# A four-layer graph network: seven groups of four dense and three listed node tiles in place of eight of four and two

## The chip, the core and the metric

The kernel runs on one core of a Trainium2 chip. The engines that matter are PE (TensorE, the matmuls; its weight loads are shown as PEld), DVE (VectorE), ACT (ScalarE), POOL (GpSimd, which here issues every gather and scatter) and SP (SyncE, which issues the plain loads and stores). The metric is the device time of one launch in microseconds (us), the median over several runs.

## The reference

A graph of 6,250 nodes with 128 features and 100,000 edges, sorted by destination, passes through four message-passing layers, each with a residual and a layer norm. The change touches the first and the third.

```python
# first layer
msg = x[src]
summed = jax.ops.segment_sum(msg, dst, num_segments=n)
mean = summed / jnp.maximum(cnt, 1.0)[:, None]
out = mean @ W_l + b_l + x @ W_r
...
# third layer: five steps of a gated unit, state h of 256 features
def step(h, Wl):
    m = h @ Wl
    agg = jax.ops.segment_sum(m[src], dst, num_segments=n)
    gi = agg @ w_ih.T + b_ih
    gh = h @ w_hh.T + b_hh
    ...
    r = jax.nn.sigmoid(ir + hr)
    z = jax.nn.sigmoid(iz + hz)
    ng = jnp.tanh(in_ + r * hn)
    h_new = (1.0 - z) * ng + z * h
    return (h_new, None)
h, _ = jax.lax.scan(step, h, W)
```

The sum over edges, `segment_sum(m[src], dst)`, is the costly part: six times in all, once for `x` and five times for the growing state.

## The kernel before

The 6,250 nodes are padded to 49 tiles of 128. A sum over edges is made for each tile of destination nodes in one of two ways.

- **Dense.** Four tiles (512 destination nodes) are one group. Its adjacency, 49 source tiles by 512 columns, is counted once in the first layer (`subtile`, line 872: one-hot matmuls in strips of U = 12 destination nodes, copied by ACT into `stage`) and kept in DRAM as bf16 (`adj_d`). A sum is then 49 matmuls of 512 columns for each part of the source table. In the first layer there are three bf16 parts (`dense0`, line 899, matmul at L904). In the third layer the table is held as two fp32r halves, for one block of 128 features in the first of the five steps and two in the others (`dense2`, line 1355, matmul at L1366): 98 matmuls in that first step and 196 in the others. The adjacency comes back from DRAM two source tiles at a time (`ab_load`) and ACT casts it to fp32r (`ab_cast`, L1337).
- **Listed.** One tile's edges lie in a list of SLOTS = 18 slots of 128 edges. For each slot POOL gathers the 128 source rows from DRAM (`gather`, L751), DVE makes a one-hot of the destinations (L1388), and one matmul adds them (`sparse0`, L935; `sparse2`, L1398). The gathers run AHEAD = 6 slots in advance in the third layer, into seven buffers. A gathered row is 2 KB there (1 KB in the first of the five steps), and 768 bytes in the first layer.

`steps` lists the chunks in node order: four dense tiles, two listed tiles, eight times, and tile 48 alone as a listed one. So 32 tiles are dense in eight groups and 17 are listed, in nine chunks.

The third layer (lines 1297 to 1597) is called the gated stage below, and its five steps are its layers 0 to 4. After the sum of a chunk come its gates (`gates`, fp32 matmuls at L1450, 48 per chunk in layers 1 to 4 and half of that in layer 0, as wide as the chunk), then the chunk's new state is turned back to rows (`rows`) and stored into the next layer's table `tab`. A gather of the next layer waits for all of that table. The weights that mix W and w_ih, `wf`, are loaded per layer (`wf_load`) into one of two buffers. The source table `hs` is reloaded in seven pieces as the last dense group of a layer finishes with each (`hs_load`).

The order of work is written by hand. Each action gets a time, `play` sorts the actions by it, and the instructions go onto every engine's queue in that order. One unit of that time is one dense group, called a round here: T = 8 rounds per layer. In the gated stage, within a layer:

- dense group d runs from d to d + 1, its gates from d + 1.005 to d + 1.305, its rows from d + 1.36;
- the listed slots start at S0 = 0.6 (0 in layer 0) and run at 36 slots per SR = 0.9 rounds (0.93 in layer 0); a listed chunk's gates come 0.05 to 0.17 after its last slot;
- the records of the fourth graph layer are scattered to DRAM by POOL as filler (`scatter`, L1535, 782 in all): from layer 1 on behind four of every seven slots, and BETWEEN = 30 behind the last slots of each layer but the last, each of these after a small memset;
- `wf` of the next layer is loaded at 6.5, the last piece of `hs` at 8.5, and the gathers of the next layer start at 8 + 0.55.

The first layer is pipelined in the same way: while group d's adjacency is counted, group d - 1 is summed by `dense0`, the listed slots run beside both, and `post` makes the layer's output rows for each chunk.

Of the kernel before, what the change touches and what calls it, by code (L numbers as in the profile page):

```python
# [15 lines left out]
P = 128  # L16
# [643 lines left out]
def even(ctx: ExitStack, tc: tile.TileContext, a, out, rec_d, start_d, list_d, rc):  # L660
# [32 lines left out]
    steps = [r for t in range(0, NT - 1, 6) for r in (range(t, t + 4), range(t + 4, t + 6))] + [range(NT - 1, NT)]  # L693
    dense, sparse = steps[0:16:2], steps[1::2] + steps[16:]
# [81 lines left out]
    with tc.tile_pool(name="f0", bufs=1) as l0, \  # L776
# [34 lines left out]
        for i, ts in enumerate(sparse):  # L811
# [3 lines left out]
            for j in range(len(ts)):  # L815
                for to, k in ((src_l, 0), (dst_l, 1)):
                    nc.sync.dma_start(to[:, 2 * i + j, :], list_d[k, bass.ds(at[j], SLOTS * P)]
                                      .rearrange("(p s) -> p s", p=P))
        first_l = l0.tile([P, len(listed)], F32, name="first_l")
        nc.gpsimd.iota(first_l[:, :16], pattern=[[6 * P, 8], [P, 2]], base=4 * P, channel_multiplier=0,  # L820
                       allow_small_or_imprecise_dtypes=True)
        nc.gpsimd.memset(first_l[:, 16:], float((NT - 1) * P))
# [11 lines left out]
        each = -(-DW // U)  # L834
        blocks = [(d, ts[0] * P // U + u, min(SU, each - u)) for d, ts in enumerate(dense) for u in range(0, each, SU)]
# [36 lines left out]
        def subtile(d, b, u, after):  # L872
# [6 lines left out]
            w = min(U, DW - c)  # L879
            p = ps(f"adj_p{b}_{u}", "adj", 2, 1024)  # L880
            for j, ohk in enumerate(hot.pop((b, u))):
                for q in range(2):
                    nc.tensor.matmul(p[:, q * 512:q * 512 + KH * U], ohss[b][:, 2 * u + j, :],  # L883
                                     ohk[:, q * KH * U:(q + 1) * KH * U], start=(j == 0), stop=(j == 1))
            nc.scalar.copy(stages[d][:, :, c:c + w].rearrange("p (q b) d -> p q b d", q=2),  # L885
                           p.rearrange("p (q n) -> p q n", q=2)[:, :, :KH * U]
                           .rearrange("p q (b d) -> p q b d", d=U)[:, :, :, :w])
# [53 lines left out]
        def turned0(t):  # L941
            ts = steps[chunk_of[t]]
            if t == ts[0]:
                aggT[ts] = l0.tile([P, 2 * P], F32, tag="aT0s", bufs=2, name=f"aT0s_{t}")
# [5 lines left out]
        def post(ts, at, by):  # L950
# [8 lines left out]
            def load():  # L959
                h["xr"] = xr = l0.tile([P, 4, D], F32, tag="xr", bufs=3, name=f"xr{r0}")  # L960
                if ts[-1] == NT - 1:
                    nc.vector.memset(xr[:, m - 1, :], 0.0)
                    nc.sync.dma_start(xr[:last, m - 1, :], a["x"][(NT - 1) * P:N, :])
                else:
# [68 lines left out]
        with tc.manual_schedule(engines=FOUR):  # L1033
# [13 lines left out]
            for d in range(len(dense)):  # L1047
# [14 lines left out]
                events += post(dense[d], d + 2.02, d + 2.95 if d < 7 else d + 2.5)  # L1062
            for k in range(len(hots)):
                t = 0.3 + 8.2 * (k + 0.5) / len(hots)
                events.append((t, lambda k=k: sparse0(k)))
                i, j = hots[k]
                if j == SLOTS - 1:
                    events.append((t + 0.05, lambda i=i: turned0(listed[i])))
                    ts = steps[chunk_of[listed[i]]]
                    if listed[i] == ts[-1]:  # L1070
                        events += post(ts, t + 0.08, t + 1.0 if i < 13 else t + 0.6)

            for c in range(NC3):
                w0, w1 = (c * K3 + KFULL, (c + 1) * K3) if c < NC3 - 1 else (c * K3, W3)
                events.append((0.5 + c * 0.5, lambda w0=w0, w1=w1: nc.sync.dma_start(
# [223 lines left out]
    with tc.tile_pool(name="f2", bufs=1) as l2, \  # L1299
# [14 lines left out]
        BETWEEN = 30  # L1314
# [6 lines left out]
        def ab_load(layer, d, g):  # L1321
            if g >= NG2:
                layer, d, g = (layer, d + 1, g - NG2) if d < 7 else (layer + 1, 0, g - NG2)
# [6 lines left out]
        def ab_cast(layer, d, g):  # L1330
            if g >= NG2:
                layer, d, g = (layer, d + 1, g - NG2) if d < 7 else (layer + 1, 0, g - NG2)
# [18 lines left out]
        def wf_load(layer):  # L1351
            wfs[layer] = wf = l2.tile([P, 2, 6 * D], F32, tag="wf", bufs=2, name=f"f_wf{layer}")
# [878 lines left out]
```

## Time and profile before

| | us |
|---|---|
| median of the runs | 7822.81 (7804.96 to 7860.64, 3 runs) |
| the profiled execution, its own time | 6785.85 |
| its span, first to last instruction | 6784.0 |
| mean granted TensorE clock in it | 0.925 |

The profiled execution stands 13% below the median of the runs; nothing in the span accounts for that. The stages lie in the span as follows:

| stage | from | to | granted clock |
|---|---|---|---|
| preparation | 0 | 150 | 1.00 |
| first graph layer | 150 | 895 | 0.93 to 0.99 |
| second graph layer | 895 | 1990 | 0.69 |
| gated stage (third graph layer) | 1990 | 5540 | 0.97 |
| its output layers, fourth graph layer | 5540 | 6784 | 0.97 |

In the gated stage, POOL starts the first and the last gather of each layer at these times:

| layer | first gather | last gather | between them | to the next layer's first |
|---|---|---|---|---|
| 0 | 1961.3 | 2418.3 | 457 | 65 |
| 1 | 2482.8 | 3208.4 | 726 | 56 |
| 2 | 3264.5 | 3980.8 | 716 | 57 |
| 3 | 4037.5 | 4764.9 | 727 | 57 |
| 4 | 4821.8 | 5516.4 | 695 | |

To read the groups of the profile: a line is the engine's line of code, operation, output and inputs by name, number of instructions, then their busy time, the mean of one in ns, and the idle time of the engine just before them with what ended it. [...] the time of one there is longer than the distance from one to the next.

### The profile page before, as it was taken

The numbers are of one execution on the slowest core, as the hardware profiler recorded it, in microseconds if no ns is written. First come the engines' busy times: TensorE is split into PE (matmuls) and PEld (weight loads), VectorE is DVE, ScalarE is ACT, GpSimd is POOL, SyncE is SP. The second block draws the span as 40 slices with busy tenths as digits, with TensorE's granted clock in tenths as the row PEclk, the third lists the DMA queues.
The fourth block names the chain that finished last, engine by engine and source line by source line (L and its number), as shares of the span: only waits on it lengthen the run. The fifth ranks groups of instructions, "written<-read, shape, count | busy, mean of one in ns | idle before, by whom it ended". The sixth has DMA issues, their size and how long they took to land.

```text
span 6784.0 us, 83554 instructions
## 1 busy us (share of the span) xinstructions
PE 5785.0 (85%) x25602; PEld 4010.0 (59%) x25758; DVE 2946.3 (43%) x8835; ACT 2406.6 (35%) x3623; POOL 4264.2 (63%) x4426
## 2 busy tenths in 40 slices
PE   0699977788859989999999989999899987888888
PEld 0355546555546657666676667666676665665665
DVE  7666634466624422222222222222222235677766
ACT  0344411111116543333333333333333323444444
POOL 3555447777756656656666666666666622777776
PEclk9999976777759999999999999999999998999999
DMA  5688744444458888778777787778777743444443
GB/s 172 162 235 244 252 139 143 140 133 137 125 170 267 264 294 258 247 226 290 255 254 232 246 294 255 242 228 298 229 239 220 230 153 101 105 108 107 110 107 82
DMA packets 804250, 1355.75 MB, mean 200 GB/s; under 512 B 165854, under 2 KB 429139, under 8 KB 802771
## 3 DMA queue, kind: packets, MB, share of 16 engines
q1 hardware_dynamic: 555219, 698.41, 32.4%
q0 software_dynamic: 207472, 568.37, 28.0%
q10 hardware_dynamic: 41104, 83.51, 3.2%
q8 instruction: 211, 3.46, 0.2%
q14 instruction: 244, 2.00, 0.1%
HBM read 1046.51 MB, written 303.32 MB: 199 GB/s over the span
## 4 chain that ended last, share of the span: by engine, by line
PE 39%; DMA 13%; POOL 4%; DVE 4%; issue 3%; ACT 1%; SPq 0%; DVEq 0%; ACTq 0%; POOLq 0%
PE ag_p L1366 16%; DMA m<-tab,src_l 5%; PE r L1450 5%; DMA f_m<-by_dst,f_ix 5%; PE z L1450 5%; PE sp_p L1398 4%; PE h L1450 2%; POOL f_m L751 2%; PE i L1450 2%; POOL rec_d L1535 1%; DVE f_m L1734 1%; PE f_y_p L1623 1%; DMA ab<-adj_d 1%; DMA rec_d<-f_rec,row 1%; PE s_p L1822 1%
## 5 line engine op out<-in xcount | busy, mean ns | idle before, releaser
L1366 PE MATMUL ag_p<-af,hs 128*128 128x512 f32 x7056 | 2105.0, 422 | 82.5 <-DMA ab<-adj_d 35.6
L751 POOL DMA_INDIRECT m<-tab,src_l x1530 | 1479.5, 967 | 1061.9 <-PE ag_p L1366 483.9
L1366 PEld LDWEIGHTS ag_p<-af,hs 128*128 128x128 f32 x7056 | 1329.3, 194 | 493.4 <-issue 136.3
L1337 ACT CAST af<-ab 128x1024 fp32r<-128x1024 bf16 (+1 forms) x1000 | 1023.2, 1028 | 990.5 <-PE ag_p L1366 636.9
L751 POOL DMA_INDIRECT f_m<-by_dst,f_ix x819 | 795.4, 971 | 304.1 <-issue 225.5
L751 POOL DMA_INDIRECT fm<-f_hw,turned_hw x782 | 781.6, 1000 | 247.0 <-issue 97.5
L1535 POOL DMA_INDIRECT rec_d<-f_rec,row x782 | 778.3, 995 | 236.9 <-issue 206.2
L1398 PE MATMUL sp_p<-m,s 128*128 128x512 f32 (+1 forms) x1530 | 685.0, 448 | 168.1 <-DMA m<-tab,src_l 162.7
L1388 DVE TENSOR_SCALAR s<-iota_h,loc_l 128x128 fp32r<-128x128 f16 x1530 | 420.7, 302 | 778.2 <-PE sp_p L1398 774.9
L1287 PE MATMUL sum<-fs,fm 128*128 128x128 f32 (+13 forms) x1924 | 453.4, 373 | 205.2 <-DMA fm<-f_hw,turned_hw 138.7
L751 POOL DMA_INDIRECT m<-x_in,src_l x306 | 356.5, 1165 | 339.8 <-PE sp_p L935 153.7
L1287 PEld LDWEIGHTS sum<-fs,fm 128*128 128x128 f32 x1924 | 368.3, 266 | 322.4 <-DVE fs L1278 133.1
L1398 PEld LDWEIGHTS sp_p<-m,s 128*128 128x128 f32 x1530 | 296.0, 193 | 345.0 <-issue 197.4
L883 PE MATMUL adj_p<-ohk,ohs 128*128 128x300 bf16 x1376 | 240.3, 298 | 121.8 <-DMA recs<-rec_d 83.8
L1464 DVE SCALAR_TENSOR_TENSOR r<-h,fc_b_hh,r 128x256 f32<-128x256 f32 (+2 forms) x170 | 101.7, 600 | 518.8 <-PE h L1450 466.2
L904 PE MATMUL ag_p<-stage,xs 128*128 128x512 bf16 x1116 | 312.0, 388 | 16.3 <-DMA xs<-x_in 8.9
L1781 ACT ACTIVATE f_hs<-dT,fc_eb 128x512 f32<-128x512 f32 (+1 forms) x208 | 148.8, 715 | 498.9 <-DVE dT L1779 498.9
L885 ACT CAST stage<-adj_p 128x600 bf16<-128x600 f32 (+1 forms) x344 | 224.8, 655 | 267.2 <-PE adj_p L883 263.3
L1472 ACT ACTIVATE z<-z,f_brz 128x256 f32<-128x256 f32 (+2 forms) x170 | 96.7, 569 | 597.9 <-PE z L1450 535.5
L1257 ACT COPY f_rec<-ap_p 128x512 f32<-128x512 f32 x196 | 105.2, 589 | 555.6 <-issue 336.6
L1481 DVE TENSOR_TENSOR r<-hold,ng 128x256 f32<-128x256 f32 (+2 forms) x153 | 84.4, 552 | 461.9 <-ACT ng L1474 460.1
L1278 DVE TENSOR_SCALAR fs<-f_iota_n,loc,turned_wgt 128x128 f32<-128x128 f32 x782 | 243.8, 355 | 94.7 <-PE sum L1287 93.9
(368 smaller groups left out, 8966.5 us busy)
## 6 DMA issues: line engine op xcount, KB each, us to landing
ab<-adj_d SPq DMA_DIRECT2D x960, 256.0 KB
f_rec<-edge_d SPq DMA_DIRECT2D x391, 130.0 KB
rg<-rec_d SPq DMA_DIRECT2D x195, 260.0 KB
edge_d<-f_rec SPq DMA_DIRECT2D x97, 520.0 KB
adj_d<-stage SPq DMA_DIRECT2D x8, 6272.0 KB
tab<-r ACTq DMA_DIRECT2D x196, 256.0 KB
hs<-tab SPq DMA_DIRECT2D x28, 1792.0 KB
xs<-x_in SPq DMA_DIRECT2D x56, 672.0 KB
```

The source lines that it names most:

```text
L751: nc.gpsimd.indirect_dma_start(out=dst, out_offset=None, in_=table, in_offset=bass.IndirectOffsetOnAxis(ap=idx, axis=0))
L883: nc.tensor.matmul(p[:, q * 512:q * 512 + KH * U], ohss[b][:, 2 * u + j, :], ohk[:, q * KH * U:(q + 1) * KH * U], start=(j == 0), stop=(j ...
L885: nc.scalar.copy(stages[d][:, :, c:c + w].rearrange("p (q b) d -> p q b d", q=2), p.rearrange("p (q n) -> p q n", q=2)[:, :, :KH * U] .rea ...
L904: nc.tensor.matmul(sums["d", d], parts[d, g][:, s % XG, q, :], stages[d][:, s, :], start=(s == 0 and q == 0), stop=(s == NT - 1 and q == 2))
L1278: nc.vector.tensor_scalar(s, iota_n, loc[:, k:k + 1], wgt[:, k:k + 1], op0=ALU.is_equal, op1=ALU.mult)
L1287: nc.tensor.matmul(sums[c][:, x0 - c0:x1 - c0], msg, s[:, x0 - w0:x1 - w0], start=False, stop=(k == last_k[c]))
L1337: nc.scalar.copy(af[:, :m, :], abs_.pop((layer, d, g))[:, :m, :])
L1366: nc.tensor.matmul(sums[layer, d, k], hs[:, s, q, k, :], afs[layer, d, g][:, s % SG, :], start=(s == 0 and q == 0), stop=(s == NT - 1 and ...
L1388: nc.vector.tensor_scalar(s, iota_h, loc_l[:, i, j:j + 1], None, op0=ALU.is_equal)
L1398: nc.tensor.matmul(p[:, :2 * w], hot.pop((layer, k)), msgs.pop((layer, k))[:, :2 * w], start=(j == 0), stop=(j == SLOTS - 1))
L1450: nc.tensor.matmul(p[:, :n], w[:, k, ms], src, start=(start and i == 0), stop=(stop and i == len(ks) - 1))
L1535: st = nc.gpsimd.indirect_dma_start(out=rec3_d, out_offset=bass.IndirectOffsetOnAxis(ap=row3[:, c:c + 1], axis=0), in_=recs[c // CB][:, c ...
```

## The change

The groups become seven, of four dense and three listed tiles each. 7 times 7 is 49, so no tile is left over: 28 tiles are dense in seven groups, 21 are listed in seven chunks. The schedule's constants follow: T is 7 rounds, 54 slots per 0.948 rounds (1.0 in layer 0), a scatter behind every second slot, 24 scatters between layers. A group now starts at a node that is no multiple of 12, so the strips of `subtile` are cut at both ends of the group; seven groups have 303 strips, eight had 344. The tiles of the listed chunks grow from two to three node tiles. `wf` has one buffer in place of two and is loaded at 7.6, which is 0.6 rounds into the next layer, behind the last gates of the layer before. `first_l`, `tiles_i` and the loading of the last rows of `x` are rewritten for the new groups.

```diff
-    steps = [r for t in range(0, NT - 1, 6) for r in (range(t, t + 4), range(t + 4, t + 6))] + [range(NT - 1, NT)]
-    dense, sparse = steps[0:16:2], steps[1::2] + steps[16:]
+    steps = [r for t in range(0, NT, 7) for r in (range(t, t + 4), range(t + 4, t + 7))]
+    dense, sparse = steps[0::2], steps[1::2]
...
-        each = -(-DW // U)
-        blocks = [(d, ts[0] * P // U + u, min(SU, each - u)) for d, ts in enumerate(dense) for u in range(0, each, SU)]
+        blocks = []
+        for d, ts in enumerate(dense):
+            b0, b1 = ts[0] * P // U, -(-(ts[0] * P + DW) // U)
+            blocks += [(d, b, min(SU, b1 - b)) for b in range(b0, b1, SU)]
...
-            w = min(U, DW - c)
+            c0, c1 = max(c, 0), min(c + U, DW)
...
             for k in range(len(hots)):
-                t = 0.3 + 8.2 * (k + 0.5) / len(hots)
+                t = 0.3 + 7.2 * (k + 0.5) / len(hots)
...
-                events.append((0.5 + c * 0.5, lambda w0=w0, w1=w1: nc.sync.dma_start(
+                events.append((0.5 + c * 0.4, lambda w0=w0, w1=w1: nc.sync.dma_start(
...
-        BETWEEN = 30
+        BETWEEN = 24
...
-            wfs[layer] = wf = l2.tile([P, 2, 6 * D], F32, tag="wf", bufs=2, name=f"f_wf{layer}")
+            wfs[layer] = wf = l2.tile([P, 2, 6 * D], F32, tag="wf", name=f"f_wf{layer}")
...
-        S0, SR = 0.6, 0.9
+        S0, SR = 0.6, 0.948
...
-            T = 8
+            T = 7
...
-                    add(o + 8.5, lambda layer=layer: hs_load(layer + 1, 6))
-                    add(o + 6.5, lambda layer=layer: wf_load(layer + 1))
+                    add(o + 7.5, lambda layer=layer: hs_load(layer + 1, 6))
+                    add(o + 7.6, lambda layer=layer: wf_load(layer + 1))
                 s0 = S0 if layer else 0.0
-                per = SR if layer else 0.93
+                per = SR if layer else 1.0
...
-                    t = o + s0 + per * (k + 0.5) / 36
+                    t = o + s0 + per * (k + 0.5) / 54
...
-                    if layer and k % 7 in (0, 2, 4, 6) and k + AHEAD < len(hots) and scattered < NK:
+                    if layer and k % 2 == 0 and k + AHEAD < len(hots) and scattered < NK:
...
-                        add(o + s0 + per * 8.32 + 0.4 * k / BETWEEN, lambda c=scattered: scatter(c, True))
+                        add(o + s0 + per * 6.83 + 0.4 * k / BETWEEN, lambda c=scattered: scatter(c, True))
```

## The prediction

> **What bounds the kernel now.** I read the page's engine shares and stage windows first, since the change touches two stages, then the groups, then the timeline of POOL and PE.
>
> ```profile
> PE 5785.0 (85%) x25602; PEld 4010.0 (59%) x25758; DVE 2946.3 (43%) x8835; ACT 2406.6 (35%) x3623; POOL 4264.2 (63%) x4426
> ...
> L751 POOL DMA_INDIRECT m<-tab,src_l x1530 | 1479.5, 967 | 1061.9 <-PE ag_p L1366 483.9
> L1535 POOL DMA_INDIRECT rec_d<-f_rec,row x782 | 778.3, 995 | 236.9 <-issue 206.2
> ```
>
> By busy time PE looks like the bound and POOL looks free. The idle column corrects that: the 782 scatters have 236.9 us of idle before them, 0.30 us each, and nothing ended it ("issue"). The timeline shows that this gap is part of the price:
>
> ```profile
> 2151.66 0.95 POOL L751 DMA_INDIRECT m<-tab,src_l  x1 [0.30 <-PE r L1450]
> 2152.92 0.95 POOL L751 DMA_INDIRECT m<-tab,src_l  x1 [0.30 <-issue]
> 2154.17 0.94 POOL L751 DMA_INDIRECT m<-tab,src_l  x1 [0.30 <-issue]
> ...
> 2648.13 0.97 POOL L751 DMA_INDIRECT m<-tab,src_l  x1 [0.30 <-PE ag_p L1366]
> 2649.41 0.99 POOL L1535 DMA_INDIRECT rec_d<-f_rec,row  x1 [0.30 <-issue]
> 2650.70 0.97 POOL L751 DMA_INDIRECT m<-tab,src_l  x1 [0.30 <-DMA m<-tab,src_l]
> ```
>
> Starts are never closer than 1.25 us (gathers alone) or 1.28 (gathers with scatters). Now the rounds, as windows:
>
> ```profile
> core 0: us, PE busy (x) PEld busy (x) DVE busy (x) ACT busy (x) POOL busy (x), PEclk, DMA share, GB/s
> 418.50:501.00 82.50, 75.93 (x413) 43.26 (x420) 57.33 (x176) 39.65 (x69) 43.90 (x38) 1.00 0.83 244
> 2151.00:2202.00 51.00, 46.50 (x199) 32.45 (x198) 23.59 (x70) 33.55 (x46) 36.09 (x39) 1.00 0.84 271
> 2514.00:2605.00 91.00, 88.80 (x353) 64.05 (x352) 26.48 (x73) 34.95 (x46) 62.96 (x65) 1.00 0.78 254
> 2985.00:3089.00 104.00, 96.61 (x380) 68.74 (x380) 27.63 (x76) 36.27 (x50) 64.81 (x66) 1.00 0.73 232
> ```
>
> First graph layer (row 1): 38 x 1.25 = 48 of 82.5 us on POOL; PE leads. Gated layer 0 (row 2): 39 x 1.25 = 49 of 51; POOL is the bound. Layer 1 (row 3): 65 x 1.28 = 83 of 91 on POOL, PE 89 of 91; both nearly full. Row 4 is a round in which a listed chunk's gates fall on top of a dense group's; its PE work is little more, and it takes 104.
>
> PE's own price comes from its timeline:
>
> ```profile
> 2609.88 1.88 PE L1450 MATMUL r<-aT,f_wf 128*128 128x512 f32 x4
> 2611.20 1.49 PE L1366 MATMUL ag_p<-af,hs 128*128 128x512 f32 x4
> 2612.52 1.88 PE L1450 MATMUL h<-hold,fw_w_hhT 128*128 128x512 f32 x4
> ...
> 2622.66 0.40 PE L1398 MATMUL sp_p<-m,s 128*128 128x512 f32 x1
> 2622.89 1.10 PE L1366 MATMUL ag_p<-af,hs 128*128 128x512 f32 x4
> 2623.82 0.39 PE L1398 MATMUL sp_p<-m,s 128*128 128x512 f32 x1
> ```
>
> Four dense matmuls take 0.93 us (0.235 each, and so does a listed one); four gate matmuls with four dense ones take 2.64, so a gate matmul of 512 columns costs 0.43, and by width (an estimate) 0.215 at 256 and 0.32 at 384. A round of layer 1: 196 x 0.235 = 46, 40 slots x 0.235 = 9.4, dense gates 48 x 0.43 = 20.6, listed gates 48 x 0.215 / 0.9 = 11.5, transposes 1.7: 89, as row 3 shows.
>
> **The change in layers 1 to 3.** PE per layer: one dense group less, -46; 72 more slots, +17; the gates keep their 49 x 128 columns, 0. So PE falls by 29. ACT loses 25 casts of 1.03 us and DVE gains 72 one-hots of 0.30; both idle beside this (ACT busy 35 of 91, DVE 26), so they count nothing unless PE and POOL both fell under about 40 a round. POOL: gathers 306 to 378, scatters between them 171 to 186: from 306 x 1.275 + 171 x 1.29 = 611 to 722, in a stretch that lasted 716 to 727. That is +111 on POOL for -29 on PE.
>
> A round of 57 slots (54 / 0.948) then needs 57 x 1.275 + 28.5 x 1.29 = 109.5 on POOL, and on PE 46 + 13.4 + 20.6 + 48 x 0.32 / 0.948 (16.3) + 2 = 98.5. The two do not overlap perfectly: between gates a slot passes PE every 1.05 us (3.44 dense matmuls and its own) and POOL every 1.92, and six gathers of lead cover only part of a stretch. With 16.5 slots in each of two such stretches, POOL needs (16.5 - 6) x 1.92 + 3 = 23, PE 17.6 (the chain shows landings of 4 to 7.5 us; 3 of it late is the value that fits the small waits of row 3): 5.5 us late, 11 a round. So 110 to 114; I take 112. The stretch from first to last gather is 0.948 x 7 = 6.64 rounds, 744; its floor is 722. The gap to the next layer was 57; it now holds 0.375 round: dense 17, gates 28, slots and transposes 3, the store's landing 5: 53. The 24 scatters with their memsets (24 x 1.6 = 38) fit in it. Layer: 797 against 782, 774 and 785 (mean 780): **+17 each, +51**; bounds -10 and +40.
>
> **Layer 0.** PE per slot is half, so POOL decides: 378 x 1.255 = 474. The old stretch was 457 for 306 x 1.255 = 384; its 73 over the floor were the start (20) and two last rounds with the reload of `hs`. Longer rounds leave the reload more room; I keep 38 of them: 512, **+55**, and the gap -10: **+45**; bounds +20 (no excess but 5) and +80 (all of it).
>
> **Layer 4.** Its 128 remaining scatters end after 256 slots: 4.5 rounds x 112 + 2.14 x 99 = 716 against 695; less than I can separate from PE's saving at the end: **+10**; bounds -20 and +20.
>
> **First graph layer.** PE leads. A round goes (43 strips x 4 x 0.13 + 147 x 0.215 = 54; bursts of 4 and 3 in its timeline); each remaining one gets 16 more slots (2.6) and a seventh tile of `post` (1.3 to 2). Eight rounds of 82.8 become seven of 89: -39. The head, before any `dense0`, holds 38 slots x 1.25 on POOL in place of 28: +10. **-29**; bounds -50 and 0. POOL, at 54 x 1.25 = 68 of 89, is the cover.
>
> **Queues and `wf`.** SP: 125 fewer `ab` loads, 41 fewer strips, 8 more list loads at 0.5 us, 7 fewer `xs` loads; it only gains room. The one `wf` buffer waits for the old layer's last gates (7.40) and is issued at 7.6; behind it on SP stand the `ab` loads, six groups ahead. First use is at 8.0: 0.4 round, 40 us, for 768 KB, 3 us at 254 GB/s. Cost 0, at worst 5 a layer. The rewritten `xr`, `first_l` and output chunks (17 to 14): -3.
>
> **Sum** on the profiled execution: 51 + 45 + 10 - 29 - 3 = **+74**, 6860 against 6786 (+1.1%). The median of the runs is 15% above that execution, and the trace does not say why; how the sum carries over depends on it. The trace's clock in this stage is 1.00 in most rounds. [...] +74 x 1.15 = +85. [...] I take the first, since the trace itself shows POOL's bound.
>
> **Rivals.**
> 1. *PE stays the bound* (faster). If PE in the timed runs is slower than in the trace, POOL's added 111 fit under it. [...] For it: 85% PE busy, the chain's first share is PE's (39%), and the 15%. Against: layer 0's gathers stand 1.25 apart. It decides from PE work of about 1.12 times the trace's.
> 2. *DMA* (slower still). Per layer 72 x 256 KB more gathered, 6.4 MB less adjacency: 196 MB (251 GB/s x 780 us) to 208, 261 GB/s at 797 us, where single rounds of the windows reached 324. If landing grows from 5 to 8 us, six gathers cover less: about +25 a layer more, 8020.
> 3. *Nothing*: POOL's excess is absorbed by the now regular spacing of gates (0.948 keeps them apart from the dense ones, and such rounds took 90, not 104): 7822 plus or minus 40.
>
> **Numbers.** POOL-bound 0.45, PE-bound 0.29, DMA 0.12, nothing 0.14. The forecast is 7822.81 + 85, about 7905; its own range, 20 to 140 more, is 7840 to 7965. The range 7690 to 8050 takes in rivals 1 and 3 and the DMA case in part. One per cent (78 us) is about what the measurement tells from none. The POOL case lies over it in 0.6 of its chance; so slower 0.27 + 0.12 = 0.39, plus 0.03 for a slow nothing: 0.42; faster 0.25 of rival 1 and 0.05 of rival 3: 0.30; within 0.28.
>
> **What would show it.** Right: gathers of layers 1 to 3 from first to last in 730 to 760, layer 0 in 495 to 535, starts at the 1.25 and 1.28 floor through most of a round, PE's wait for `m` up from 227 us. Wrong: stretches under 716 (my 1.28 is no floor), PE busy above 95% in these rounds (rival 1), or gathers landing over 8 us late (rival 2).

## The result, and the profile after

| | us | ratio to before |
|---|---|---|
| before, in the runs beside it | 7827.07 (7804.96 to 7860.64, 4 runs) | |
| changed kernel | 8027.87 (8004.35 to 8048.95, 4 runs) | 1.0252, interval 1.0205 to 1.0299 |

The change makes the kernel slower by 2.5%; the prediction said 1.1% (7905). This one-core kernel takes 6776 us on one of the five chips that the experiments ran on and 7732 to 7823 (medians) on the other four, and the profile ahead of the prediction, 6786, is of the first kind, while the result and most experiments are of the second. "The quick chip" below is that one chip. A profile of before of the second kind was therefore taken first (experiment 0), and the profile after is compared with that.

The heads and groups of after answer to those shown of before:

```profile
PE 6006.5 (75%) x24202; PEld 3952.5 (49%) x24353; DVE 2983.2 (37%) x9049; ACT 2239.7 (28%) x3337; POOL 4675.3 (58%) x4833
...
L751 POOL DMA_INDIRECT m<-tab,src_l x1890 | 1824.5, 965 | 1412.4 <-PE ag_p L1368 449.9
...
L1400 PE MATMUL sp_p<-m,s 128*128 128x512 f32 (+1 forms) x1890 | 927.8, 497 | 377.7 <-DMA m<-tab,src_l 225.0
...
L1537 POOL DMA_INDIRECT rec_d<-f_rec,row x782 | 779.7, 997 | 260.7 <-issue 233.6
```

The listed matmuls of before, in experiment 0:

```profile
L1398 PE MATMUL sp_p<-m,s 128*128 128x512 f32 (+1 forms) x1530 | 690.0, 451 | 108.4 <-DMA m<-tab,src_l 65.4
```

The means of these matmuls (497 and 451 ns) are longer than the distance from one start to the next: in the prediction's timeline one at 2622.66 shows 0.40 us, and the next starts 0.23 us behind it. The 360 more gathers are there (1890 for 1530), each at the old price (965 ns for 967). PE's idle time just before its listed matmuls (`sp_p`) rose from 108 to 378 us, most of it ended by a message that lands (`m`). But neither engine is fuller: PE is at 75%, POOL at 58%. The windows from the first to the last gather of layers 1 to 3 show the same; first after, then before of the same kind (experiment 0). The columns are the stretch, its length, each engine's busy time, the granted clock, the DMA share and GB/s.

```profile
2839.00:3705.00 866.00, 701.07 (x2379) 456.60 (x2378) 200.57 (x575) 227.36 (x296) 554.79 (x570) 0.91 0.73 233
3776.00:4640.00 864.00, 707.70 (x2378) 462.69 (x2378) 200.75 (x575) 227.14 (x295) 553.62 (x570) 0.90 0.73 233
4711.00:5565.00 854.00, 712.59 (x2396) 468.21 (x2396) 203.52 (x577) 229.53 (x296) 557.57 (x570) 0.91 0.74 236
```

```profile
2696.00:3520.00 824.00, 709.29 (x2612) 500.74 (x2613) 189.58 (x524) 257.80 (x338) 467.04 (x476) 0.93 0.71 227
3591.00:4412.00 821.00, 706.34 (x2614) 501.08 (x2613) 187.82 (x524) 257.29 (x338) 467.32 (x476) 0.93 0.71 228
4483.00:5302.00 819.00, 703.52 (x2614) 497.99 (x2614) 187.89 (x524) 257.10 (x338) 466.99 (x476) 0.94 0.71 228
```

The old stretches are 820, not the 716 to 727 of the first profile, and the new ones 854 to 866, not 744. The prediction's floors for POOL (611 before, 722 after) lie 130 to 210 us below them, so POOL's rate alone does not set them. What else does is seen in what engines wait for. In after, from the first gather of layer 1 to the last of layer 3 (total, number, longest; us):

```profile
PEld sp_p L1400 <- issue: 304.8, 370, 7.3
...
ACT af L1339 <- remote: 207.8, 29, 15.0
...
DVE s L1390 <- remote: 110.1, 30, 9.0
POOL m L751 <- remote: 95.5, 51, 3.4
```

"Remote" means that the signal that ended the wait came more than 1.5 us after the end of any instruction that gives it. The timeline of before (experiment 0) shows one such place. The last column is the idle time before, and what ended it:

```profile
2939.43 1.10 PE L1366 MATMUL ag_p<-af,hs 128*128 128x512 f32 x4
2939.90 0.29 DVE L1388 TENSOR_SCALAR s<-iota_h,loc_l 128x128 fp32r<-128x128 f16 x1 [4.77 <-PE ag_p L1366]
...
2941.21 0.97 POOL L751 DMA_INDIRECT m<-tab,src_l  x1 [0.30 <-issue]
2942.49 0.95 POOL L751 DMA_INDIRECT m<-tab,src_l  x1 [0.30 <-issue]
2943.74 0.99 POOL L1535 DMA_INDIRECT rec_d<-f_rec,row  x1 [0.30 <-issue]
2944.78 0.28 DVE L1388 TENSOR_SCALAR s<-iota_h,loc_l 128x128 fp32r<-128x128 f16 x1 [4.59 <-remote]
2944.78 1.04 ACT L1337 CAST af<-ab 128x1024 fp32r<-128x1024 bf16 x1 [5.74 <-remote]
...
2950.10 1.22 PE L1366 MATMUL ag_p<-af,hs 128*128 128x512 f32 x2 [9.58 <-ACT aT L1373]
```

PE's last matmul ends at 2940.53. DVE and ACT both wait for a matmul to be finished and both start at 2944.78, on one signal that comes 4.2 us late; POOL meanwhile issues at its pace. PE starts again at 2950.10, behind work of ACT that had itself waited, 9.6 us after it stopped. In the trace's list of semaphore updates, those of PE often come in bursts, under 60 ns behind one another; in the first profile they come 234 ns apart at the median, as the matmuls start, and none under 60. The bursts' share, from the first gather of layer 1 to the last of layer 3, is 24% in before and 33% in after. In the first profile of before, and in all four traces of the quick chip, it is 0, and no wait is put down to "remote" there.

### The profile page after: what moved, and what is told of

Read it like the earlier page. It is cut to its first block, busy times and chain, and to the rows that moved or that the text cites. A ratio compares the mean times of both kernels' runs of the same rounds, so it can differ in the third digit from the quotient of the medians.

```text
span 8021.3 us, 81042 instructions
## 1 busy us (share of the span) xinstructions
PE 6006.5 (75%) x24202; PEld 3952.5 (49%) x24353; DVE 2983.2 (37%) x9049; ACT 2239.7 (28%) x3337; POOL 4675.3 (58%) x4833
## 4 chain that ended last, share of the span: by engine, by line
PE 56%; issue 13%; another core or an unknown queue 8%; DMA 8%; DVE 6%; POOL 3%; ACT 3%; SPq 1%; ACTq 0%; DVEq 0%; POOLq 0%
PE ag_p L1368 13%; PE r L1452 5%; DMA m<-tab,src_l 5%; PE z L1452 5%; PE sp_p L1400 5%; PE sum L1289 3%; PE s_p L1824 3%; PE m_p L1789 2%; PE h L1452 2%; PE i L1452 2%; PE h_p L1774 2%; POOL m L751 2%; PE ag_p L905 2%; PE adj_p L884 1%
## 5 line engine op out<-in xcount | busy, mean ns | idle before, releaser
L751 POOL DMA_INDIRECT m<-tab,src_l x1890 | 1824.5, 965 | 1412.4 <-PE ag_p L1368 449.9
L1368 PE MATMUL ag_p<-af,hs 128*128 128x512 f32 x6174 | 1993.9, 445 | 238.4 <-ACT aT L1375 100.5
L1339 ACT CAST af<-ab 128x1024 fp32r<-128x1024 bf16 (+1 forms) x875 | 889.7, 1027 | 1546.8 <-PE ag_p L1368 526.0
L1400 PE MATMUL sp_p<-m,s 128*128 128x512 f32 (+1 forms) x1890 | 927.8, 497 | 377.7 <-DMA m<-tab,src_l 225.0
L1400 PEld LDWEIGHTS sp_p<-m,s 128*128 128x128 f32 x1890 | 395.6, 209 | 696.7 <-issue 523.9
L1781 DVE TENSOR_TENSOR dT<-h_p,dT 128x512 f32<-128x512 f32 (+1 forms) x208 | 141.4, 680 | 433.0 <-remote 131.6
L1789 PE MATMUL m_p<-f_hs,fw_L_gnn_eW 128*128 128x512 f32 (+1 forms) x416 | 245.8, 676 | 71.4 <-ACT mT L1791 29.0
L1824 PE MATMUL s_p<-f_s,f_ms 128*128 128x128 f32 (+1 forms) x1638 | 285.8, 319 | 12.4 <-issue 12.2
L1466 DVE SCALAR_TENSOR_TENSOR r<-h,fc_b_hh,r 128x384 f32<-128x384 f32 (+1 forms) x140 | 95.1, 683 | 524.4 <-PE h L1452 223.1
L886 ACT CAST stage<-adj_p 128x600 bf16<-128x600 f32 x303 | 196.6, 652 | 319.4 <-PE adj_p L884 181.6
```

Source lines behind the costliest of these rows:

```text
L751: nc.gpsimd.indirect_dma_start(out=dst, out_offset=None, in_=table, in_offset=bass.IndirectOffsetOnAxis(ap=idx, axis=0))
L1339: nc.scalar.copy(af[:, :m, :], abs_.pop((layer, d, g))[:, :m, :])
L1368: nc.tensor.matmul(sums[layer, d, k], hs[:, s, q, k, :], afs[layer, d, g][:, s % SG, :], start=(s == 0 and q == 0), stop=(s == NT - 1 and ...
L1400: nc.tensor.matmul(p[:, :2 * w], hot.pop((layer, k)), msgs.pop((layer, k))[:, :2 * w], start=(j == 0), stop=(j == SLOTS - 1))
L1789: nc.tensor.matmul(p_m[:, :e], e2[:, 0, :], held[i].pop("hs")[:, :e], start=True, stop=True)
L1824: nc.tensor.matmul(sums[c][:, a0:a1], ms[:, j * P:(j + 1) * P], s[:, :a1 - a0], start=False, stop=(stop and j == m - 1))
```

## The experiments

"Stretch" is the time from first to last gather of a layer, "period" that to the next layer's first gather (mean of layers 1 to 3), "late signals" the sum of all waits ended by "remote" from the first gather of layer 1 to the last of layer 3, all engines together (waits of several engines for one signal count more than once, so it is no measure of lost time).

| kernel | ratio to before on the same chip | period, us | late signals, us |
|---|---|---|---|
| before (0) | | 890 | 522 |
| changed kernel (result; 4; 16) | 1.025; 1.025; 1.032 | 932; 931; 919 | 673; 680; 588 |
| changed kernel without scatters in the stage (1) | 1.092 | 768 | 54 |
| before without scatters in the stage (2) | 1.061 | 735 | 0 |
| before, loads one block later (5) | 0.999 | 899 | 567 |
| before, 72 tiny gathers more per layer (7) | 1.040 | 964 | 844 |
| before, deeper lead (8) | 1.003 | 905 | 686 |
| before, 72 slots more without gathers (9) | 1.002 | 895 | 484 |
| four dense, one listed (10) | 0.972 | 836 | 115 |
| before with memsets (11; 17) | 0.985; 0.989 | 869; 870 | 329; 400 |
| first profile of before, of the quick kind | | 780 | 0 |
| quick chip: 72 gathers of 16 rows (12) | 1.028 | 811 | 0 |
| quick chip: 72 direct loads (13) | 1.009 | 779 | 0 |
| quick chip: changed kernel with memsets (14) | 1.060 | 854 | 0 |
| quick chip: one listed, with memsets (15) | 1.026 | 795 | 0 |

**0. Before once more**, no edit.

> The kernel before, unchanged, for a profile in the state of its timed runs (7827), since the profile on record is of 6786 and that of after, 8021, is at its median. If the 15% is the machine's, the stage that neither kernel changes (second graph layer, 1095 in the first profile) is longer here as it is in after's profile (from 944 to 2155), and layers 1 to 3 of the gated stage take about 780 x 1.15 = 897 each, against 930 to 937 in after. If the profile comes again at 6786, the comparison of stages stays unsafe.

7745.23 us, one run, beside a median of 7732.26 in 23 runs. The work is the same, instruction for instruction; the stretches are 820 long, at a granted clock of 0.93 in place of 0.98.

**1 and 2. Without the filler.** All 782 scatters go behind the last gather of the stage, in the changed kernel and in before.

```diff
-                    if layer and k % 2 == 0 and k + AHEAD < len(hots) and scattered < NK:
-                        add(t + 1e-6, lambda c=scattered: scatter(c))
-                        scattered += 1
...
+            for c in range(NK):
+                add(LAYERS * T + 9, lambda c=c: scatter(c, True))
+                scattered += 1
```

> The changed kernel with all 782 scatters moved out of the gated stage's loop, behind its last gather (each with its memset, about 1.6 us: some 1,250 us are added at the end). Theory POOL (gathers and scatters together fill POOL): the stretches from first to last gather of layers 1 to 3, 854 to 866 with scatters, fall by 100 or more. Rival PE or machine stalls: they fall by less than 40, since POOL was not what they waited for. Rival DMA: they fall by the scatters' share of bytes, under 10%, 30 to 60.

> The kernel before with its scatters moved in the same way. Theory POOL: its stretches fall by 50 or less from those of the kernel before in the same state (POOL was 92% full, PE 98%), and the changed kernel without filler is then no slower than this one in layers 1 to 3 (29 us less PE work a layer); in total it differs by under 1%, layer 0 being slower and the rest faster. Rival DMA or lists as such: it is still slower by 2% or more.

8432.95 us (ratio 1.092, 1.0887 to 1.0954) and 8201.24 (1.0614, 1.0589 to 1.0639). The scatters, now alone at the end, cost more in all. (In the first profile a scatter behind its memset starts 1.28 us after the one before it; the 1.6 of the prediction and of (1) was too high an estimate.) But the stretches fell by 150 in the changed kernel (from 857 in experiment 4 to 707, layer 1), as the theory of POOL had it, and by 135 in before (825 to 689), where the expectation of before had at most 50. So the filler is not free in before either. Before, first layer 1:

```profile
2683.00:3372.00 689.00, 667.22 (x2622) 484.38 (x2621) 190.00 (x524) 259.52 (x339) 293.42 (x305) 0.99 0.71 239
```

PE is busy 667 of 689 now: before is PE's once the scatters are out, and the late signals are gone (0 from 522). The second half of the expectation was missed too, and it is the half that bears on the change: the changed kernel should then have been no slower in layers 1 to 3. It is slower by 32 us in each, as with the filler (4 against 5, on one chip: 33), and by 2.8% in all (8433 against 8201). Its stretches of 707 to 712 are far above what its 378 gathers need on POOL alone (378 x 1.255 = 474), and its late signals are 54. So a difference of this size needs neither POOL's floor nor many late signals. PE's waits for messages in layers 1 to 3, before and the changed kernel without scatters:

```profile
PE sp_p L1398 <- DMA m<-tab,src_l: 20.3, 4, 7.1
```

```profile
PE sp_p L1400 <- DMA m<-tab,src_l: 60.1, 57, 6.7
```

**3. One buffer for the gate weights**, in before.

```diff
-            wfs[layer] = wf = l2.tile([P, 2, 6 * D], F32, tag="wf", bufs=2, name=f"f_wf{layer}")
+            wfs[layer] = wf = l2.tile([P, 2, 6 * D], F32, tag="wf", name=f"f_wf{layer}")
...
-                    add(o + 6.5, lambda layer=layer: wf_load(layer + 1))
+                    add(o + 8.6, lambda layer=layer: wf_load(layer + 1))
```

> The kernel before with the one buffer for the fused gate weights alone, loaded at 8.6, 0.6 rounds into the next layer. My prediction: no difference, under 0.3% (the load has 0.4 of a round before its first use). Rival: the wait for the weights holds PE at each of four layer starts by 10 us or more, 0.5% or more slower.

7741.74 us, ratio 1.0019 (1.0003 to 1.0035). This part of the change costs some 15 us (2 to 27 by the interval).

**4, 5 and 6. SyncE's queue.** The changed kernel once more (4), and before (5) and the changed kernel (6) with the scatters' records loaded one block later, so that SyncE waits less for a free buffer with the adjacency loads behind it.

```diff
-                rec_load(c // CB + 3)
+                rec_load(c // CB + 2)
...
-            for b in range(3):
+            for b in range(2):
```

> The changed kernel, unchanged, on the same chip as the following ones: a ratio near 1.025 and a profile in the ordinary state, for comparison stage by stage with the kernel before in that state. All theories: gated layer 0 about 615 from first to last gather, layers 1 to 3 about 860.

> The kernel before with the records for a scatter loaded two blocks ahead and not three, so that on SP's queue a load waits for a scatter that POOL issued four to seven slots earlier and not for the newest one. Theory SP (the loads of records hold SP to POOL's pace, the adjacency loads behind them come late, ACT's casts and then PE wait): SP's waits for rec_d, 300 to 400 us in a layer, fall by half or more, and layers 1 to 3 fall from about 890 towards the 737 that they take without scatters; 2 to 5% faster. Theory POOL alone (its rate is the bound): under 0.5% of change. Rival: the records now come too late for the scatters and POOL waits for them: slower by 1% or more.

> The same edit in the changed kernel. Theory SP: it gains as in the kernel before or more, and its distance to that one shrinks. Theory POOL: no gain over 0.5%, since 722 us of issues stay in each of layers 1 to 3.

8026.16 us (ratio 1.0248), 7809.62 (0.9986, 0.9971 to 1.0001) and 8028.32 (1.0250). No gain. The premise was missed too: SyncE's waits for the scatters, some 286 us a layer in experiment 0, are 267 in (5), not half, and in layer 1 of the changed kernel they are 305 (4) and 308 (6). So this edit did not free SyncE, and what its order costs stays untested.

**7. 72 tiny gathers more per layer**, in before: 128 rows of 8 bytes each, that nothing reads.

```diff
+        def tiny(layer, k):
+            i, j = hots[k]
+            gather(l2.tile([P, 2], F32, tag="tiny", bufs=3, name=f"tiny{layer}_{k}"), rec_d, src_l[:, i, j:j + 1])
...
+                    if k % 17 in (0, 4, 8, 12):
+                        add(t + 5e-7, lambda layer=layer, k=k: tiny(layer, k))
```

> The kernel before with 72 more gathers in each of the five layers, one behind four of every 17 slots, of 8 bytes a row into a tile that nothing reads: POOL's count of the changed kernel, with next to none of its bytes and none of its PE, DVE or ACT work. Theory POOL: slower by the changed kernel's whole loss or more, +2 to +4%: layer 0 by 80 to 100 us, layers 1 to 3 by 40 to 75 each (PE saves nothing here). Rival DMA bytes: under +0.7%. Rival PE or slots as such: under +0.7%.

8153.97 us, ratio 1.0396 (1.0354 to 1.0439): 331 us for 360 gathers, 0.92 us each, with no bytes to speak of and nothing on PE. Layers 1 to 3 grow by 65 each against (5) on the same chip. ACT's wait for late signals alone doubled, and PE's waits for ACT and DVE rose from 119 us in (5) to 238. PE's wait for messages hardly moved (38 to 51), so this kernel loses its time behind other waits than the changed kernel does. ACT's wait in layers 1 to 3 of before (experiment 0), then in this kernel:

```profile
ACT af L1337 <- remote: 177.5, 31, 9.2
```

```profile
ACT af L1337 <- remote: 354.7, 53, 17.2
```

**8. A deeper lead**, in before with one buffer for the weights: AHEAD = 9 in place of 6.

> Before with one buffer for the gate weights (which cost nothing) and the gathers of the second graph layer started nine slots ahead instead of six. If TensorE's waits for messages (162 us and more in the list of waits) are a matter of lead, three more slots of lead are about 7 us on each of the gathers and the gated layers fall by some 20 us each, 1 to 1.5% in all. If it is GpSimd's number of issues that decides, the lead moves the waits but not the rate at which messages come: within 0.4% of before.

7829.04 us, ratio 1.0031 (1.0016 to 1.0046). In before the lead is not short; but PE hardly waits for messages there (some 40 us in layers 1 to 3), and a deeper lead in the changed kernel was not run.

**9. 72 slots more per layer without gathers**, in before with one buffer: a second one-hot and a second matmul on a message that is there already. Some edges count twice, so its sums are not the reference's.

```diff
+            if k % 17 in (0, 4, 8, 12):
+                hot[layer, k, "x"] = s = l2.tile([P, P], F32R, tag="Sx", bufs=4, name=f"sx_{layer}_{k}")
+                nc.vector.tensor_scalar(s, iota_h, loc_l[:, i, j:j + 1], None, op0=ALU.is_equal)
...
+                nc.tensor.matmul(p[:, :n], hot.pop((layer, k, "x")), msg[:, :n], start=False, stop=False)
```

> Before with one buffer for the gate weights and 72 more slots per gated layer on VectorE and TensorE alone: a second one-hot tile and a second matmul on a message that is already there, no gather (some edges count twice in the sums). If the slot as such is dear, on TensorE or VectorE, this costs nearly what the 72 gathers without their matmuls cost, 3.5 to 4.5%. If GpSimd's issues are what is dear, only TensorE's price is left, 72 x (0.235 to 0.45) us = 17 to 32 us per gated layer, 85 to 160 us in all, 1.1 to 2.0%.

7824.69 us, ratio 1.0024 (1.0009 to 1.0040), of which the one buffer may be most; both expectations were higher. On this chip 360 more matmuls and one-hots cost nothing that can be told: PE has 115 us of idle time a layer (experiment 0) to put them in. On the quick chip, where PE is busy for 678 of 726 us (first profile, layer 1), this was not run.

**10. The change turned round**: nine groups of four dense tiles and one listed, and a last group of four; two buffers for the weights. The scatters follow at five for every four slots, one in five of them behind a small memset.

```diff
-    steps = [r for t in range(0, NT - 1, 6) for r in (range(t, t + 4), range(t + 4, t + 6))] + [range(NT - 1, NT)]
+    steps = [r for t in range(0, NT - 4, 5) for r in (range(t, t + 4), range(t + 4, t + 5))] + [range(NT - 4, NT)]
...
-        S0, SR = 0.6, 0.9
+        S0, SR = 0.6, 1.06
...
-            T = 8
+            T = 10
```

> The change turned round: nine groups of four dense tiles and one listed, and a last group of four, so 40 tiles by the adjacency and 9 by lists; two buffers for the gate weights; 144 gathers fewer per layer than before. At some 0.92 to 1.17 us per gather GpSimd's price falls by 132 to 168 us a layer, and eight more dense tiles cost about 92 us in each gated layer (two thirds of what four fewer saved, turned round): 40 to 80 us less per gated layer, 200 to 400 us less in all five, less what ten rounds of the first graph layer take more than eight: 7450 to 7750 us, ratio 0.95 to 0.99. If the number of issues is not what decides and TensorE is, the eight dense tiles cost 92 to 125 us a layer against 144 slots x 0.235 to 0.45 us = 34 to 65 us: 1 to 4% slower than before.

7580.98 us, ratio 0.9720 (0.9691 to 0.9749). It beats both kernels here. Its layer 1:

```profile
2751.00:3491.00 740.00, 709.62 (x2868) 505.64 (x2867) 149.94 (x384) 297.94 (x391) 352.80 (x394) 0.98 0.65 210
```

PE carries 256 more matmuls than before in this stretch (2868 for 2612), and yet the stretch is 84 us shorter, at a clock of 0.98 for 0.93: late signals fell from 522 us to 115. What part the small memsets have in it was not separated.

**11 and 17. POOL's time without gathers**, in before: four small memsets at each of the places of the 72 tiny gathers (the edit is shown against that of experiment 7).

```diff
-            gather(l2.tile([P, 2], F32, tag="tiny", bufs=3, name=f"tiny{layer}_{k}"), rec_d, src_l[:, i, j:j + 1])
+            for _ in range(4):
+                nc.gpsimd.memset(apart_by, 0.0)
```

> Before with four tiny GpSimd memsets in the place of each of the 72 tiny gathers per gated layer: 0.30 us each from start to start, 1.2 us for four, as much of GpSimd's time as a gather with the gap behind it (1.25 to 1.28 us), and no DMA. If it is GpSimd's time that the gated layers are short of, this costs what the tiny gathers cost, 60 to 85 us a layer, 3.5 to 4.5% in all. If it is what a gather sets going in the software DMA queue [...], the memsets cost next to nothing: under 0.7%. Between them, a share of each.

> Before with 72 times four memsets once more. On a chip where before takes some 6780 us: if GpSimd's time is what is short there, 72 x 0.8 us = 58 us a layer, ratio 1.03 to 1.045; if not, within 1%. On a chip where before takes 7740 to 7830: ratio 0.98 to 0.99 if the gain of the first time was no accident of that chip.

7625.42 us, ratio 0.9849 (0.9801 to 0.9897), and on another chip 7648.01, ratio 0.9889 (0.9866 to 0.9911). Both expectations of (11) were missed, and with them the theory that a gather costs by POOL's time. Four memsets take less than the 1.2 us expected: a gather starts 2.09 us after the one before in place of 1.28, so 0.81 for four, 58 us of POOL a layer. Yet the kernel became faster, on two chips. In before, on these chips, POOL's time is not short, and with the memsets the late signals fell from 522 us to 329 and 400. The changed kernel, with 72 gathers more, was not run with memsets there. Why memsets do this was not found; that they spread gathers and scatters out in time is a guess.

**12 to 15. On the quick chip.** 72 gathers of 16 rows in place of 128 (12, shown against experiment 7); 72 direct loads of 128 rows of 8 bytes from SyncE (13); the changed kernel (14) and the kernel of experiment 10 (15) with four memsets behind 89 and 38 gathers per layer.

```diff
-            gather(l2.tile([P, 2], F32, tag="tiny", bufs=3, name=f"tiny{layer}_{k}"), rec_d, src_l[:, i, j:j + 1])
+            gather(l2.tile([P, 2], F32, tag="tiny", bufs=3, name=f"tiny{layer}_{k}")[:16, :], rec_d, src_l[:16, i, j:j + 1])
...
+            nc.sync.dma_start(l2.tile([P, 2], F32, tag="tiny", bufs=3, name=f"tiny{layer}_{k}"), tab[0][:P, :2])
...
+                    if k % 17 in (0, 4, 8, 12):
+                        add(t + 5e-7, still)
```

> Before with 72 more gathers per gated layer, as in the run with the tiny gathers, but of 16 rows of 8 bytes in place of 128. [...] If it is dear as an indirect instruction with its issue and its semaphores, it stays at 3.3 to 4.5%.

> Before with 72 direct loads of 128 rows of 8 bytes per gated layer from SyncE's queue, in the place of the tiny gathers[...]. [...] If it is the software queue or GpSimd's indirect instruction, within 0.7%.

> The changed kernel with four tiny GpSimd memsets behind 89 of the 378 gathers of each gated layer. If holding GpSimd back a little is what gained 1.5% in before, and it does the same here, 0.5 to 2% faster than the changed kernel, ratio to before 1.005 to 1.02. If the changed kernel is held by GpSimd's own time, 89 x 0.8 us = 71 us per layer come on top: ratio 1.05 to 1.07.

> Groups of four dense tiles and one listed, with four tiny GpSimd memsets behind 38 of the 162 gathers of each gated layer. GpSimd has room there (45% busy), TensorE is full: if the memsets help by pacing gathers and scatters, up to 1% faster than without them (ratio to before 0.96 to 0.972); if they helped before only because gathers came too close together, nothing here: 0.969 to 0.975.

Before took 6776.19 us beside them (7 runs). 6953.20 us, ratio 1.0275 (1.0251 to 1.0299); 6834.99, 1.0093 (1.0070 to 1.0116); 7178.88, 1.0600 (1.0574 to 1.0627); 6950.64, 1.0264 (1.0242 to 1.0286).

(12) costs 0.49 us a gather. That lies between an eighth of the 0.92 us of (7), for a price that goes by rows, and the whole of it, for one that goes by instructions, and since (12) ran on another kind of chip than (7) it can't tell the two apart; by the packets of POOL's queue each tiny gather is 16 packets of data in both (of 64 bytes in (7), of 8 in (12)) and 16 of 4 bytes. (13) costs nothing in layers 1 to 3 (779 against 780), so small loads from another queue are not dear there; its 59 us fall in layer 0, whose period is 578 in place of 522. (14) is the one that comes nearest to the prediction: here memsets cost, and POOL is at its floor. POOL's timeline of (14), layer 1:

```profile
2705.00 0.97 POOL L751 DMA_INDIRECT m<-tab,src_l  x1 [0.30 <-DMA m<-tab,src_l]
2706.27 0.95 POOL L751 DMA_INDIRECT m<-tab,src_l  x1 [0.30 <-PE sp_p L1400]
2707.52 0.99 POOL L1537 DMA_INDIRECT rec_d<-f_rec,row  x1 [0.30 <-issue]
2708.82 0.97 POOL L751 DMA_INDIRECT m<-tab,src_l  x1 [0.31 <-issue]
2709.79 0.53 POOL L1546 MEMSET apart_by<- 1x1 f32 x4
2710.93 0.94 POOL L751 DMA_INDIRECT m<-tab,src_l  x1 [0.61 <-PE ag_p L1368]
```

378 x 1.275 + 186 x 1.29 + 89 x 0.81 = 794 of a stretch of 802 to 805. And PE waits for messages, as the prediction said of the bound it saw: 97 us in layers 1 to 3 of the first profile of before, 313 in (14):

```profile
PE sp_p L1398 <- DMA m<-tab,src_l: 97.1, 78, 9.8
```

```profile
PE sp_p L1400 <- DMA m<-tab,src_l: 313.4, 231, 6.7
```

(15) shows the other side, outside both of its expectations, which were set for the other kind of chip: the split that is 2.8% faster in experiment 10 is 2.6% slower here with memsets added. PE is idle for 20 us a layer in its layers 1 to 3, and waits for messages for 16 us in the three together, so the memsets can account for little of the 174 us lost; the split without them was not run here.

**16. The changed kernel a third time**, on a fifth chip, an ordinary one.

> The changed kernel once more. On a chip where before takes some 6780 us, the prediction's own sum (+74 us) asks for 6855, ratio 1.011, gathers of layers 1 to 3 in stretches of 744 us; if the price of 0.92 to 1.1 us a gather holds there as well, +200 us, ratio 1.03. On a chip where before takes 7740 to 7830: ratio 1.02 to 1.03 as in the two earlier comparisons.

7978.73 us, ratio 1.0322 (1.0294 to 1.0350). The changed kernel alone on the quick chip was not measured.

## Why the prediction was right and wrong

The direction held. The size did not: +205 us for +85 (7822.81 and 85 are 7908, put down as about 7905). "Ordinary" in the table is experiment 4 less experiment 5, which is before but for the order of some loads, on the same chip; "quick" is experiment 14 less 72 us a layer for its memsets (89 x 0.81), against the first profile, or, in the first graph layer, against experiments 12 and 13. That the memsets cost their full time there is shown by the floor above for layers 1 to 3 of (14) only.

| term | predicted | ordinary | quick |
|---|---|---|---|
| first graph layer, a round | 89 | 93.8 | 88.6 |
| first graph layer | -29 | +10 | -22 |
| layer 0, period | +45 | +100 | +60 |
| layers 1 to 3, each | +17 | +33 | +3 |
| layer 4 | +10 | +8 | -15 |
| rewritten loads and outputs | -3 | not separated | not separated |
| one buffer for the weights | 0 | +15, within the rows above | |
| sum | +74, carried over as +85 | +217 (the result itself +205) | +43 to +403 |

- **What failed** is the step "I take the first, since the trace itself shows POOL's bound": the bound of the first profile was taken for that of the timed runs, and the sum was carried over by a factor of 1.15, as if every engine were that much slower. This was the author's assumption, shown by no trace or run, and it is not so. A gather takes 965 to 968 ns in both profiles, and PE is busy for 706 us of a stretch in experiment 0 against 678 in the first profile, 4% more. Nor is POOL's floor needed for a difference of this size between the kernels: with the scatters out, the changed kernel stands some 235 us above that floor and is slower by the same 32 us a layer (1 and 2).
- **What stands in its place** is idle time of PE that ends with a message. From the first gather of layer 1 to the last of layer 3, PE is busy for 2,224 us in (5) and 2,223 in (4), and idle for 404 and 500. So the saving of 29 us of PE work a layer, a term of the sum, does not show in its busy time. PE's waits for messages rose by 95 us, as much as its idle time; its waits for ACT rose from 73 to 126, and the ones that the profile can't name fell from 246 to 179. First (5), then (4):

```profile
PE sp_p L1398 <- DMA m<-tab,src_l: 38.1, 16, 7.7
```

```profile
PE sp_p L1400 <- DMA m<-tab,src_l: 133.3, 103, 7.0
```

- **Late signals** go with the loss but don't measure it: 522 us in before, 673 in the changed kernel, 844 with the tiny gathers; but without scatters the kernels differ by the same 32 us a layer at 0 and 54, and the deeper lead (8) has 686, more than the changed kernel, at a period of 905. Why PE comes to wait for messages in a kernel whose POOL is not full stays open.
- **POOL as the bound** of layers 1 to 3 fits the quick chip: in (14) PE waits for messages and POOL stands at its floor, and less its memsets the stretch is 730 to 733, where 744 was predicted. But (14) has 72 us of POOL's time a layer more than the changed kernel, so that the changed kernel itself is bound by POOL there is not shown. POOL as the bound was wrong for the runs that were timed: their stretches are 120 to 144 us above that floor, and of the marks that were named they miss 730 to 760. PE's wait for messages is up, as named: 303.5 us in the whole gated stage (225.0 before matmuls, 78.5 before weight loads) from 227 in the first profile; and against 65.4 in experiment 0, of the same kind of chip, the rise is larger.
- **Layer 0** was mis-sized: +100 for +45, outside its upper bound of 80. The prediction let the stretch's excess over POOL's floor shrink from 73 to 38 us. On the ordinary chip it was 118 in before (5) and became 135 (4). Layer 0 holds no scatters between its gathers, and with them out of the stage (1 against 2) it still grew by 96; 72 tiny gathers cost it 84. PE's granted clock in it is 0.80 in the changed kernel, and 0.90 in before on the same kind of chip (experiments 0 and 5); whether that is a cause or comes of PE's waits was not separated. The changed kernel's layer 0, in the columns above:

```profile
2155.00:2770.00 615.00, 432.81 (x1447) 274.38 (x1448) 188.94 (x567) 234.68 (x295) 362.38 (x383) 0.80 0.68 216
```

- **The first graph layer** was right on the quick chip. On the others, the share of PE's updates that come in bursts rose from about 1% in before to between 15 and 20% in the changed kernel, and rounds took 93.8. Whether the bursts are the cause was not tested.
- **Layer 4, the queues and the weights' buffer** were right within their bounds (3; 5 and 6).
- **A slot's price on PE**, 0.235, was too high if anything on an ordinary chip: nothing that can be told (9).
- **Rival 1** (PE stays the bound, faster) fell: PE is idle for 141 to 165 us of each stretch of layers 1 to 3. **Rival 2** named 8020, near the 8028 measured, but by luck, for the landing of transfers does not carry it. By the packets of POOL's queue (the 4-byte ones, 16 to each gather or scatter, taken in order) a gather of layers 1 to 3 has landed 3.7 us after its start in (5) and 3.6 in (4) at the median, 5.7 and 5.6 at nine in ten, none over 8; the DMA share is 0.73 against 0.71. **Rival 3** fell with the sign.

Open stay: why the changed kernel's PE waits longer for messages on the ordinary chips; what holds the late signals back, and why five chips differ in it; whether a gather's rows or its instruction set its price (12 could not tell); and what memsets do. Every run on record has its span and clock recorded, so none shows these kernels unrecorded: that the recording itself plays a part in the late signals can't be excluded.

## What to carry to other kernels

Before a sum is made on a profile whose own time is far from the timed runs, take another profile that is not; a factor between them can't stand for a wait that one of them doesn't have. Price a gather by adding gathers that nothing reads, and an engine's time by adding time on that engine: in before, on ordinary chips, the one cost 4% and the other gained 1%, while busy shares said that both were free. Then compare which waits grew, for the added gathers cost by other waits than the change did. Where a split between two ways is tuned by hand, the best split can differ between chips: four dense and one listed won 2.8% on one and, with memsets added, lost 2.6% on another.

## What was not expected of the hardware

- The same program, with gathers of the same duration (967 and 968 ns) and 4% more busy time on PE in a layer's stretch, took 6776 us on one chip and 7732 to 7823 on four.
- On those four, 24 to 34% of PE's semaphore updates in layers 1 to 3 of before and the changed kernel came under 60 ns behind another. In layer 1 of experiment 0 the gaps ahead of such bursts are 0.5 to 3.5 us. The trace there holds 4,819 of the 6,208 updates that PE's instructions of layers 1 to 3 give; the first profile holds 6,206 of 6,207, with no bursts. Bursts and missing records alone cost nothing that can be told: before without scatters (2) has 8% in bursts and 4,534 of 6,215 on record, with 0.4 us of late waits.
- In layer 1 of the changed kernel (2839 to 3705, mean granted clock 0.91) PE has 22 idle times over 2 us (2.0 to 9.2), and 18 of them are followed, 1.5 to 4.8 us behind their start, by a stretch at a granted clock of 0.5, 3.4 to 13.7 us long; five more such stretches have no such pause ahead. In this order the lower clock comes after the waiting; whether it comes of it was not tested.
- Four POOL memsets of one element between two gathers add 0.81 us to the distance of their starts (0.146 us from one memset to the next), and on two ordinary chips made before 1.1 to 1.5% faster.
